# Feed-forward activations issued in another order, and attention keys written by two activations over all partitions

## The chip, the cores and the metric

The kernel runs on one core of a Trainium2 chip. The metric is the device time of one execution in microseconds (us), the median over several executions. One core has TensorE (matrix products into PSUM), VectorE, ScalarE (activations), GpSimd and DMA queues; each works through its own queue of instructions, and they wait for each other by semaphores. Profile lines call them PE, DVE, ACT and POOL; PEld is TensorE's loading of weights.

## The reference

128 graphs of 128 nodes with 256 features each go through two layers; everything is float32. Cut to what matters:

```python
# layer 0: two graph attention steps, then a feed-forward
def _gat(h, adj, W, a, out_features):
    Wh = jnp.matmul(h, W)
    e = jnp.matmul(Wh, a[:out_features]) + jnp.swapaxes(jnp.matmul(Wh, a[out_features:]), 1, 2)
    scores = jnp.where(adj > 0, jax.nn.leaky_relu(e, negative_slope=0.2), NEG)
    return jnp.matmul(jax.nn.softmax(scores, axis=1), Wh)

h = _gat(_gat(x, adj, W1, a1, 256), adj, W2, a2, 256)
h = _layernorm(x + h, g_ln1, b_ln1)
ff = jnp.matmul(jax.nn.relu(jnp.matmul(h, w_ff1) + b_ff1), w_ff2) + b_ff2     # 256 -> 1024 -> 256
src = _layernorm(h + ff, g_ln2, b_ln2)

# layer 1: attention of 8 heads of 32, values by relation r = 0..3, then a feed-forward
q, k = heads(src @ Wq + bq), heads(src @ Wk + bk)
attn = jax.nn.softmax(jnp.einsum('bhid,bhjd->bhij', q, k) / np.sqrt(32), axis=-1)
out = sum(jnp.einsum('bhij,bhjd->bhid', attn * (adj == r)[:, None], heads(src @ Wv[r] + bv[r])) for r in range(4))
x = _ln(src + out @ Wo + bo, g1, beta1)
ff = jax.nn.gelu(x @ W1 + b1, approximate=False) @ W2 + b2                   # 256 -> 1024 -> 256
return _ln(x + ff, g2, beta2)
```

## The kernel before

The 128 graphs go in 32 groups of 4. Each group passes through five stages (load, graph attention, feed-forward with Relu, attention, feed-forward with Gelu), and the stages of neighbouring groups are interleaved: each stage is a generator that yields an estimated duration, and a heap decides whose next piece is written into the program. The order of TensorE's instructions (and of the DMA queue's) is then fixed by added dependencies over most of the kernel; the orders on the other engines are chosen when the kernel is built, from the order of the program and from what is estimated to be ready.

PSUM holds eight buffers of 128x512 values; six are called `mm` and are used in turn by nearly all products.

```python
ps = ctx.enter_context(tc.tile_pool(name="ps", bufs=6, space=PSUM))
...
kbd = [cst.tile([P, G, 2, N], F32, name=f"kbd{c}") for c in range(DC)]
for c in range(DC):
    nc.gpsimd.memset(kbd[c], 0.0)
...
def normalised(y, first=0, n=G):          # layer norm without gain and offset
    ...                                   # VectorE: bn_stats, bn_aggr; GpSimd: rstd and -mean * rstd
    for b in range(n):
        nc.scalar.activation(y[:, b], y[:, b], AF.Identity, bias=nmr[:, b:b + 1], scale=rstd[:, b:b + 1])   # L235
```

The first product of the feed-forward is done with seven block products of Strassen-Winograd form for each half, in two units (`unit(0)`, `unit(2)`), each with four visits; `chain` and `side` are PSUM buffers, `lo` and `hi` hold the results and then the activations:

```python
def unit(f0):
    lo, hi = (wk.tile([P, 2, 2, T // 2], F32, name="fT", bufs=FC // 2) for _ in range(2))
    ...
    chain, side = (ps.tile([P, 2, T // 2], F32, name="mm") for _ in range(2))
    product(chain, 1, True)
    product(side, 5, True)                # products are L303
    nc.scalar.copy(lo[:, :, 0], chain)
    nc.scalar.copy(hi[:, :, 1], side)
    yield
    p = ps.tile([P, 2, T // 2], F32, name="mm")
    product(chain, 6)
    product(p, 2, True)
    product(side, 3)
    nc.scalar.copy(lo[:, :, 1], chain)
    nc.vector.tensor_add(lo[:, :, 0], lo[:, :, 0], p)             # L317
    nc.vector.tensor_add(lo[:, :, 1], lo[:, :, 1], side)          # L318
    yield
    product(chain, 7)
    nc.vector.tensor_add(hi[:, :, 1], hi[:, :, 1], chain)         # L321
    yield
    product(chain, 4)
    for i in range(2):
        nc.scalar.activation(lo[:, i], lo[:, i], func, bias=bin_[:, f0 + i:f0 + i + 1])        # L325
    for i in range(2):
        f = FC // 2 + f0 + i
        nc.scalar.activation(hi[:, i, 1], hi[:, i, 1], func, bias=bin_[:, f:f + 1])            # L328
        nc.scalar.activation(hi[:, i, 0], chain[:, i], func, bias=bin_[:, f:f + 1])            # L329
    yield

units = [unit(0), unit(2)]
for n, now in enumerate(((0,), (1,), (0,), (1,), (0,), (1,), (0,), (1,))):
    for u in now:
        next(units[u])
    ...
...
for b2_ in range(0, G, 2):                # the second product of the feed-forward
    p = ps.tile([P, 2, D], F32, name="mm")
    for b in (b2_, b2_ + 1):
        for n, f in enumerate(late):
            nc.tensor.matmul(p[:, b - b2_], fT[f][:, ts(b, N)], wout[:, f], ...)               # L346
    nc.vector.tensor_add(y[:, b2_:b2_ + 2], y[:, b2_:b2_ + 2], p)                              # L347
```

Other products that appear in the profile are L388 (features times weights) and L396, L406 (weighting) of the graph attention, L420 (queries), L426 (keys), L441 (scores), L474 (values), L486 (weighting by relation) and L524 (output) of the attention. L467 makes the masked weights on VectorE, L397 copies the four results of L396 out of PSUM on ScalarE, and L258 transposes on VectorE.

In the attention one score product takes two heads at once. For that the keys lie in `kbd` in a block form: of every two neighbouring heads of 32 rows, one fills slot 0 and the other slot 1, and the rows of the other head are zero there. The zeros are written once, at the start; each group writes only the rows of the heads, four activations of 32 partitions for each of the two halves `c`:

```python
for c in range(DC):
    p = ps.tile([P, G, N], F32, name="mm")
    for f in range(DC):
        nc.tensor.matmul(p, wkk[:, f, ts(c, P)], hT[:, :, f], start=f == 0, stop=f == DC - 1)      # L426
    for q in range(HC):
        rows = ts(q, DH)
        nc.scalar.activation(kbd[c][rows, :, q % 2], p[rows], AF.Identity, bias=bk[rows, c:c + 1])  # L429
...
def weights(b):
    scores = [ps.tile([P, DC, 2, N], F32, name="mm") for _ in range(2)]
    for c in range(DC):
        for h in range(2):
            rows = ts(h, P // 2)
            nc.tensor.matmul(scores[h][:, c], qT[rows, c, ts(b, N)], kbd[c][rows, b], ...)          # L441
```

A float32 matmul of the program stands as two instructions in the profile, so the four of `weights(b)` are eight there.

Of the kernel before, what the change touches and what calls it, by code (L numbers as in the profile page):

```python
# [12 lines left out]
F32 = mybir.dt.float32  # L13
I32 = mybir.dt.int32
AF = mybir.ActivationFunctionType
OP = mybir.AluOpType
# [6 lines left out]
P = 128  # L23
# [34 lines left out]
def graph_layers(ctx: ExitStack, tc: tile.TileContext, a: dict, out: bass.AP):  # L58
# [8 lines left out]
    nc = tc.nc  # L67
# [5 lines left out]
    DC = D // P  # L73
    FF = a["wf1"].shape[1]
    FC = FF // P
    R = a["wv"].shape[1] // D
    H = 8
    DH = D // H
    HC = P // DH
# [3 lines left out]
    cst = ctx.enter_context(tc.tile_pool(name="cst", bufs=1))  # L83
# [55 lines left out]
    for fc in range(DC):  # L139
        p = ps.tile([P, MW], F32, name="mm")  # L140
# [27 lines left out]
    bf1, b1, bq, bk = (at_col[k] for k in ("bf1", "b1", "bq", "bk"))  # L168

    def folded(w, bias, k, rows=False):  # L170

        gain, offset = at_col["g" + k], at_col["b" + k]
        if rows:
            for n in range(0, w.shape[-1], T):
                p = ps.tile([P, T], F32, name="mm")
                for c in range(DC):
                    nc.tensor.matmul(p, offset[:, c:c + 1].to_broadcast([P, P]), w[:, c, n:n + T],
                                     start=c == 0, stop=c == DC - 1)
                nc.vector.tensor_add(bias[:, n:n + T], bias[:, n:n + T], p)
        else:  # L180
            n = bias.shape[-1]
            p = ps.tile([P, n], F32, name="mm")
            for f in range(n):
                for c in range(DC):
                    nc.tensor.matmul(p[:, f:f + 1], w[:, c, ts(f, P)], offset[:, c:c + 1], start=c == 0, stop=c == DC - 1)
            nc.vector.tensor_add(bias, bias, p)
        for c in range(DC):
            nc.vector.tensor_scalar(w[:, c], w[:, c], gain[:, c:c + 1], None, op0=OP.mult)
# [21 lines left out]


    kbd = [cst.tile([P, G, 2, N], F32, name=f"kbd{c}") for c in range(DC)]
    for c in range(DC):
        nc.gpsimd.memset(kbd[c], 0.0)

    def per_row(v, n):

# [2 lines left out]
    def normalised(y, first=0, n=G):  # L220

        y = y[:, first:first + n]
        mv = sm.tile([P, n, 2], F32, name="mv")
        for b in range(n):
            st = sm.tile([P, 6], F32, name="st")
            nc.vector.bn_stats(st, y[:, b])  # L226
            nc.vector.bn_aggr(mv[:, b], st)
        rstd = sm.tile([P, n], F32, name="rstd")
        nc.gpsimd.tensor_scalar(rstd, mv[:, :, 1], EPS, None, op0=OP.add)
        nmr = sm.tile([P, n], F32, name="nmr")  # L230
        nc.gpsimd.tensor_scalar(nmr, mv[:, :, 0], -1.0, None, op0=OP.mult)
        nc.gpsimd.tensor_tensor(rstd, rstd, mhalf[:, :n], OP.pow)  # L232
        nc.gpsimd.tensor_mul(nmr, nmr, rstd)  # L233
        for b in range(n):
            nc.scalar.activation(y[:, b], y[:, b], AF.Identity, bias=nmr[:, b:b + 1], scale=rstd[:, b:b + 1])  # L235

    def affine(y, k, b, n, engine=nc.gpsimd):


        for op, v in zip((OP.mult, OP.add), ln[k]):  # L240
            engine.tensor_tensor(y[:, b:b + n], y[:, b:b + n], v[:, None, :].to_broadcast([P, n, D]), op)  # L241
# [26 lines left out]
    def features(y, direct):  # L268

        t = t_tile().rearrange("p (b c n) -> p b c n", b=G, c=DC)  # L270
        blocks = t.rearrange("p b c n -> p (b c) n")
        transposed(y.rearrange("p b (c f) -> p (b c) f", f=P), blocks, direct, blocks)
        return t

    def moving_sums(hT):

        b11, b21, b12, b22 = (hT[:, h:h + G // 2, c] for h in (0, G // 2) for c in range(DC))
        t1, t2, t4 = (wk.tile([P, G // 2, N], F32, name=f"t{i}") for i in (1, 2, 4))
        nc.gpsimd.tensor_sub(t1, b12, b11)  # L279
        nc.gpsimd.tensor_sub(t2, b22, t1)  # L280
        nc.gpsimd.tensor_sub(b12, b22, b12)
        nc.gpsimd.tensor_sub(t4, t2, b21)
        return None, b11, b21, b22, t4, t1, t2, b12

    def feed_forward(y, before, direct, win, bin_, wout, func, by=G):


        hT = features(y, direct)
        yield TIMES["lead ff0" if before == "01" else "lead ff1"]
        hs = moving_sums(hT)  # L290
        yield TIMES["sums"]
        fT = [None] * FC
# [5 lines that stand above are left out]
                fT[f0 + i] = lo[:, i].rearrange("p h t -> p (h t)")  # L298
                fT[FC // 2 + f0 + i] = hi[:, i].rearrange("p h t -> p (h t)")

            def product(p, k, first=False):
                for i in range(2):
                    nc.tensor.matmul(p[:, i], win[k][:, ts(f0 + i, P)], hs[k], start=first and i == 0, stop=True,  # L303
                                     skip_group_check=True)

            chain, side = (ps.tile([P, 2, T // 2], F32, name="mm") for _ in range(2))
            product(chain, 1, True)
            product(side, 5, True)
# [10 lines that stand above are left out]
            yield  # L319
            product(chain, 7)  # L320
            nc.vector.tensor_add(hi[:, :, 1], hi[:, :, 1], chain)  # L321
            yield
            product(chain, 4)
            for i in range(2):
                nc.scalar.activation(lo[:, i], lo[:, i], func, bias=bin_[:, f0 + i:f0 + i + 1])  # L325
            for i in range(2):
                f = FC // 2 + f0 + i
                nc.scalar.activation(hi[:, i, 1], hi[:, i, 1], func, bias=bin_[:, f:f + 1])  # L328
                nc.scalar.activation(hi[:, i, 0], chain[:, i], func, bias=bin_[:, f:f + 1])  # L329
            yield  # L330

        units = [unit(0), unit(2)]
# [3 lines that stand above are left out]
            if n in (2, 4):  # L336
                affine(y, before, n - 2, 2)
            yield TIMES["ff unit"]
        yield TIMES["ff2"]

        late = sorted(range(FC), key=lambda f: f % (FC // 2) // 2)
        for b2_ in range(0, G, 2):
# [3 lines that stand above are left out]
                    nc.tensor.matmul(p[:, b - b2_], fT[f][:, ts(b, N)], wout[:, f], start=n == 0, stop=n == FC - 1)  # L346
            nc.vector.tensor_add(y[:, b2_:b2_ + 2], y[:, b2_:b2_ + 2], p)  # L347
            yield TIMES["ff half"]
            if (b2_ + 2) % by == 0:
                normalised(y, b2_ + 2 - by, by)  # L350
        return y
# [59 lines left out]
    def attention(y, g, first, direct):  # L411
# [5 lines left out]
        for c in range(DC):  # L417
            p = ps.tile([P, T], F32, name="mm")
# [4 lines left out]
        for c in range(DC):  # L423
            p = ps.tile([P, G, N], F32, name="mm")
            for f in range(DC):
                nc.tensor.matmul(p, wkk[:, f, ts(c, P)], hT[:, :, f], start=f == 0, stop=f == DC - 1)  # L426
            for q in range(HC):
                rows = ts(q, DH)
                nc.scalar.activation(kbd[c][rows, :, q % 2], p[rows], AF.Identity, bias=bk[rows, c:c + 1])  # L429

        adj = ps.tile([P, G, N], F32, name="adj", bufs=1)
        nc.vector.tensor_copy(adj, at)
# [74 lines left out]
        for b in range(G):  # L507
# [8 lines left out]
            for k in range(0, 8, 2):  # L516
# [4 lines left out]
                if k == 4:  # L521
                    p = ps.tile([P, D], F32, name="mm")
# [37 lines left out]
    def stage_attention(g):  # L560
        if g == 0:
            folded(wq, bq, "02")
            folded(wkk, bk, "02")
            folded(wv_all, bv, "02", rows=True)
            folded(w1, b1, "11")
            later["w1"] = weight_sums(w1, "w1")
        x2[g] = yield from attention(x1.pop(g), g, g == 0, g == NG - 1)

    def stage_ff1(g):
# [8 lines left out]
        if not last:  # L578
            yield TIMES["store"]
            nc.sync.dma_start(out[g], y)  # L580

    stages = (stage_load, -75), (stage_gat, -39), (stage_ff0, 48), (stage_attention, 132), (stage_ff1, 300)
    todo = []
    for g in range(NG):
# [74 lines left out]
```

## Time and profile before

| | |
|---|---|
| time, median of 3 runs (lowest to highest) | 3239.61 us (3239.05 to 3241.12) |
| span of the profiled execution | 3241.0 us |
| mean granted TensorE clock | 0.991 of full speed |
| instructions | 55392 |
| L325, ScalarE, 128x512, x256 | 169.3 us busy, 709 ns each |
| L328, ScalarE, 128x256, x256 | 114.2 us busy, 493 ns each |
| L329, ScalarE, 128x256 from PSUM, x256 | 103.1 us busy, 465 ns each |
| L429, ScalarE, 32x512 from PSUM, x256 | 173.9 us busy, 679 ns each |
| table loads of ScalarE | 62, 1283 ns each |
| wait of L441's weight loads for L329, in total | 32.1 us |
| wait of L303 for VectorE's L321, in total | 18.2 us |

In lists of groups each line has the line of the kernel, the engine, what is written and what is read, the tile's shape and a count; then the total busy time and the mean of one. In a timeline each line has a start in us from the start of the span, a length in us, the engine, the line, the tiles and how many instructions were merged; what stands in square brackets is idle time of the engine just before, and what ended it. The chain that ended last is followed back from the last instruction: at each step to what released it, or to the instruction before it on its engine.

### The profile page before, as it was taken

What the parts mean: (1) busy time and instruction counts of PE and PEld (TensorE: products, weight loads), DVE (VectorE), ACT (ScalarE), POOL (GpSimd) and SP (SyncE); (2) the same over time, 40 slices, a digit from 0 to 9 for tenths busy, and PEclk for the clock granted to TensorE, in tenths of its full rate; (3) what the DMA queues carried; (4) which work ended last, traced back from release to release, by engine and by line L of the source; (5) the groups of instructions that cost most, each with busy time, mean ns of one, the idle gap of its engine ahead of it and who ended that gap; (6) DMA issues with size and microseconds to landing.
All of it is one profiled execution on the core that took longest, in us unless ns stands there. A gap on an engine that the chain in (4) does not pass through costs nothing.

```text
span 3241.0 us, 55392 instructions
## 1 busy us (share of the span) xinstructions
PE 3145.3 (97%) x20160; PEld 2383.3 (74%) x20160; DVE 2020.5 (62%) x3647; ACT 1766.8 (55%) x5191; POOL 1378.8 (43%) x1736
## 2 busy tenths in 40 slices
PE   7989999999999999999999999999999999999998
PEld 5756777777777777777777777777777777777766
DVE  3566566666566666576666576666576666666563
ACT  3545555565555565555565555565555565555543
POOL 2324345344345344345344345344345344344342
PEclk8999999999999999999999999999999999999999
DMA  4344454444454444454444454444453544453310
GB/s 152 68 102 98 102 117 101 105 98 98 100 119 102 104 95 100 99 121 96 111 94 97 103 120 97 110 92 98 105 121 89 117 92 98 104 115 85 85 33 14
DMA packets 1156400, 320.83 MB, mean 99 GB/s; under 512 B 902944, under 2 KB 1126688, under 8 KB 1156000
## 3 DMA queue, kind: packets, MB, share of 16 engines
q1 hardware_dynamic: 1156128, 317.29, 43.2%
q8 instruction: 160, 2.62, 0.3%
q14 instruction: 112, 0.92, 0.1%
HBM read 187.58 MB, written 129.62 MB: 98 GB/s over the span
## 4 chain that ended last, share of the span: by engine, by line
PE 75%; POOL 9%; ACT 7%; DVE 6%; DMA 1%; issue 1%; SPq 1%; ACTq 0%; POOLq 0%; DVEq 0%
PE mm L346 28%; PE mm L303 13%; PE mm L474 10%; PE av L486 5%; POOL tok L241 5%; PE mm L441 5%; PE mm L388 3%; PE mm L420 3%; PE mm L426 3%; PE mm L524 3%; ACT fT L325 2%; ACT tok L235 2%; POOL rstd L232 2%; PE mm L406 2%; DVE st L226 1%; ACT fT L328 1%
## 5 line engine op out<-in xcount | busy, mean ns | idle before, releaser
L467 DVE SCALAR_TENSOR_TENSOR m<-adj,eT 128x1024 f32<-128x1024 f32 x512 | 598.8, 1213 | 228.5 <-DMA eT<-zd 161.9
L241 POOL TENSOR_TENSOR tok<-tok,ln_rows 128x512 f32<-128x512 f32 (+1 forms) x636 | 668.7, 1060 | 42.1 <-PE mm L252 14.8
L453 POOL TENSOR_TENSOR e<-e,s 128x512 f32<-128x512 f32 x256 | 266.1, 1040 | 706.2 <-DVE s L452 679.0
L451 ACT ACTIVATE e<-mm,nm 128x128 f32<-128x128 f32 x1024 | 360.7, 376 | 190.0 <-DVE nm L447 167.2
L474 PE MATMUL mm<-wv,T 128*128 128x512 f32 x1024 | 464.2, 596 | 0.0
L346 PE MATMUL mm<-wf,fT 128*128 128x256 f32 x2048 | 456.9, 381 | 0.0
L346 PE MATMUL mm<-w,fT 128*128 128x256 f32 x2048 | 455.5, 381 | 0.2 <-DVE v L475 0.2
L346 PEld LDWEIGHTS mm<-w,fT 128*128 128x128 f32 x2048 | 386.6, 190 | 74.6 <-issue 23.8
L346 PEld LDWEIGHTS mm<-wf,fT 128*128 128x128 f32 x2048 | 386.4, 190 | 63.3 <-ACT wh L397 9.3
L235 ACT ACTIVATE tok<-tok,nmr,rstd 128x256 f32<-128x256 f32 x512 | 269.4, 594 | 178.7 <-POOL nmr L233 166.2
L474 PEld LDWEIGHTS mm<-wv,T 128*128 128x128 f32 x1024 | 191.5, 190 | 199.6 <-issue 189.3
L347 DVE TENSOR_TENSOR tok<-tok,mm 128x512 f32<-128x512 f32 x128 | 87.8, 686 | 351.5 <-PE mm L346 351.5
L486 PE MATMUL av<-m,v 128*32 128x128 f32 x8192 | 254.8, 276 | 8.8 <-DVE v L475 4.9
L486 PEld LDWEIGHTS av<-m,v 128*32 128x32 f32 x8192 | 218.8, 111 | 54.3 <-issue 41.6
L429 ACT ACTIVATE kbd<-mm,col 32x512 f32<-32x512 f32 x256 | 173.9, 679 | 151.0 <-PE mm L426 147.0
L377 POOL TENSOR_TENSOR e<-e,s 128x512 f32<-128x512 f32 x64 | 66.5, 1039 | 432.7 <-DVE s L376 338.4
L279 POOL TENSOR_TENSOR t<-T 128x256 f32<-128x256 f32 x64 | 46.4, 726 | 466.7 <-DMA T<-zd 466.7
L451 ACT ACTIVATION_READ_ACCUMULATOR e<-mm,nm 128x1 f32 x1024 | 219.8, 215 | 0.0
L447 DVE TENSOR_REDUCE nm<-mm 128x4 f32<-128x512 f32 x256 | 162.9, 675 | 64.5 <-PE mm L441 64.5
L303 PE MATMUL mm<-T,w 128*128 128x256 f32 x768 | 197.0, 386 | 0.2 <-ACT T L256 0.2
L475 DVE TENSOR_TENSOR v<-mm,bv 128x512 f32<-128x512 f32 x256 | 167.5, 684 | 46.8 <-PE mm L474 46.8
L303 PE MATMUL mm<-T,wf 128*128 128x256 f32 x768 | 192.6, 380 | 0.0
(121 smaller groups left out, 5112.3 us busy)
## 6 DMA issues: line engine op xcount, KB each, us to landing
zd<-e SPq DMA_DIRECT2D x496, 128.0 KB, 3.1
eT<-zd SPq DMA_DIRECT2D x124, 512.0 KB, 4.0
zd<-T SPq DMA_DIRECT2D x364, 128.0 KB, 3.5
T<-zd SPq DMA_DIRECT2D x91, 512.0 KB, 3.9
xt<-in_xT_dram SPq DMA_DIRECT2D x32, 512.0 KB
at<-in_adjT_dram SPq DMA_DIRECT2D x64, 256.0 KB, 6.1
tok<-in_x_dram SPq DMA_DIRECT2D x32, 512.0 KB
out_dram<-tok SPq DMA_DIRECT2D x31, 512.0 KB, 6.5
```

Source lines behind the costliest of these rows:

```text
L235: nc.scalar.activation(y[:, b], y[:, b], AF.Identity, bias=nmr[:, b:b + 1], scale=rstd[:, b:b + 1])
L241: engine.tensor_tensor(y[:, b:b + n], y[:, b:b + n], v[:, None, :].to_broadcast([P, n, D]), op)
L303: nc.tensor.matmul(p[:, i], win[k][:, ts(f0 + i, P)], hs[k], start=first and i == 0, stop=True, skip_group_check=True)
L346: nc.tensor.matmul(p[:, b - b2_], fT[f][:, ts(b, N)], wout[:, f], start=n == 0, stop=n == FC - 1)
L429: nc.scalar.activation(kbd[c][rows, :, q % 2], p[rows], AF.Identity, bias=bk[rows, c:c + 1])
L447: nc.vector.tensor_reduce(nm, p, AX.X, OP.max, negate=True)
L451: nc.scalar.activation(eh[:, q], p[:, q], AF.Exp, bias=nm[:, q:q + 1], accum_out=s[:, q:q + 1])
L453: nc.gpsimd.tensor_mul(eh, eh, per_row(s, N))
L467: nc.vector.scalar_tensor_tensor(m, ab, r, eT, op0=OP.is_equal, op1=OP.mult)
L474: nc.tensor.matmul(p, hT[:, b, f], wv[:, f, r:r + 2], start=f == 0, stop=f == DC - 1)
L475: nc.vector.tensor_add(v[:, r:r + 2].rearrange("p r d -> p (r d)"), p.rearrange("p r d -> p (r d)"), bv[:, r * D:(r + 2) * D])
L486: last = nc.tensor.matmul(po[ts(q, DH), c], v[:, r, c * P + q * DH:c * P + (q + 1) * DH], ms[r][:, q // 2 * HC + c * 2 + q % 2], start=r = ...
```

## The change

There are two parts. In the feed-forward's units the activations of `lo` move from the last visit to the one before it, and in the last visit the two activations that read the PSUM buffer `chain` come ahead of the two that read `hi[:, :, 1]` from SBUF. This is for the PSUM buffers to come free earlier. In the attention each half of the keys is written by two activations over all 128 partitions, one for each slot, in place of four over 32. A scale of 1 or 0 for each partition (`own`) keeps the rows of the slot's own heads and writes zeros to the others; the bias is multiplied by the same numbers beforehand (`bk_own`). So the memsets of `kbd` at the start are not needed.

```diff
     kbd = [cst.tile([P, G, 2, N], F32, name=f"kbd{c}") for c in range(DC)]
-    for c in range(DC):
-        nc.gpsimd.memset(kbd[c], 0.0)
+
+    own = cst.tile([P, 2], F32, name="own")
+    nc.vector.memset(own, 0.0)
+    for q in range(HC):
+        nc.vector.memset(own[ts(q, DH), q % 2:q % 2 + 1], 1.0)
+    bk_own = [cst.tile([P, DC], F32, name=f"bk{q}") for q in range(2)]
...
             product(chain, 7)
             nc.vector.tensor_add(hi[:, :, 1], hi[:, :, 1], chain)
+            for i in range(2):
+                nc.scalar.activation(lo[:, i], lo[:, i], func, bias=bin_[:, f0 + i:f0 + i + 1])
             yield
             product(chain, 4)
-            for i in range(2):
-                nc.scalar.activation(lo[:, i], lo[:, i], func, bias=bin_[:, f0 + i:f0 + i + 1])
-            for i in range(2):
-                f = FC // 2 + f0 + i
-                nc.scalar.activation(hi[:, i, 1], hi[:, i, 1], func, bias=bin_[:, f:f + 1])
-                nc.scalar.activation(hi[:, i, 0], chain[:, i], func, bias=bin_[:, f:f + 1])
+            for h, p in enumerate((chain, hi[:, :, 1])):
+                for i in range(2):
+                    f = FC // 2 + f0 + i
+                    nc.scalar.activation(hi[:, i, h], p[:, i], func, bias=bin_[:, f:f + 1])
             yield
...
-            for q in range(HC):
-                rows = ts(q, DH)
-                nc.scalar.activation(kbd[c][rows, :, q % 2], p[rows], AF.Identity, bias=bk[rows, c:c + 1])
+            for q in range(2):
+                nc.scalar.activation(kbd[c][:, :, q], p, AF.Identity, scale=own[:, q:q + 1], bias=bk_own[q][:, c:c + 1])
...
             folded(wkk, bk, "02")
+            for q in range(2):
+                nc.vector.tensor_scalar(bk_own[q], bk, own[:, q:q + 1], None, op0=OP.mult)
```

## The prediction

> **What bounds the kernel now.** I read the shares of the engines first, then the table of 100 us stretches, then the chain that ended last over two rounds of the loop, and only then the instructions of single engines around the places where that chain leaves TensorE.
>
> ```profile
> PE 3145.3 (97%) x20160; PEld 2383.3 (74%) x20160; DVE 2020.5 (62%) x3647; ACT 1766.8 (55%) x5191; POOL 1378.8 (43%) x1736
> ```
>
> TensorE is the engine that is nearly full. From 300 us to 3000 us each 100 us shows it 98.2 to 98.9% busy at a granted clock of 1.00, so the middle of the kernel is one pattern. One group of four graphs passes every 97.48 us: the first score product after the feed-forward stands at 911.85, 1009.33 and 1106.81 us in the chain.
>
> The busy share hides something, since the ends of matmuls are modelled. The chain shows what. In order of time (start, length in us, engine, line), one round:
>
> ```profile
> 1078.41 7.12 PE mm L346 x32
> ...
> 1086.16 1.21 DVE e L370
> ...
> 1090.18 1.04 POOL e L377
> ...
> 1099.73 0.17 POOL nmr L233
> ...
> 1099.92 2.08 ACT tok L235 x4
> 1102.00 1.22 ACT fT L325 x2
> 1103.22 0.80 ACT fT L328 x2
> 1104.02 1.23 ACT fT L325 x2
> 1105.25 0.80 ACT fT L328 x2
> 1106.05 0.72 ACT fT L329 x2
> ...
> 1106.81 0.70 PE mm L441 x2
> ...
> 1107.53 1.13 PE mm L441 x6
> ```
>
> The reader should see that from the end of L346 at 1085.53 to L441 at 1106.81, 21.28 us, the chain is not on TensorE. It goes through VectorE, GpSimd's part of the layer norms, four normalising activations (L235) and ten of the feed-forward's twelve activations. TensorE works beside it, but not for the whole time. Its own instructions there:
>
> ```profile
> 1100.77 1.97 PE L303 MATMUL mm<-t,wf 128*128 128x256 f32 x8 [0.59 <-DVE fT L321]
> 1102.57 1.90 PE L396 MATMUL mm<-wh,e 128*128 128x258 f32 x8
> 1104.40 1.96 PE L486 MATMUL av<-m,v 128*32 128x128 f32 x64
> 1106.81 1.85 PE L441 MATMUL mm<-kbd,T 64*128 64x256 f32 x8 [0.46 <-ACT fT L329]
> ```
>
> Two stalls. (a) L441: L486 takes 1.89 us where nothing stops it, so L441 could start at 1106.29; it starts at 1106.81 (0.52 us), and takes 1.85 us where two undisturbed occurrences in this round take 1.06 (0.79 us more, between its first output and its second). Together 1.31 us; one round earlier 0.28 + 0.79 = 1.07. (b) The last product of the feed-forward (L303 from t and wf): the 8 matmuls of L474 before it start at 1096.58 and take 3.43, so it could start at 1100.01 and starts at 1100.77: 0.76 us, one round earlier 0.99. Both rounds lose 2.07 us, so the round needs 97.48 - 2.07 = 95.41 us of TensorE.
>
> The reason for (a) is in the code. PSUM has six "mm" buffers. Two units' `chain` and four outputs of L396 fill them, and the two score outputs of L441 take the buffers that the two `chain` give back, which L329 reads last of all twelve activations.
>
> The reason for (b) is VectorE's order; its instructions ahead of it are:
>
> ```profile
> 1094.19 0.69 DVE L317 TENSOR_TENSOR fT<-fT,mm 128x512 f32<-128x512 f32 x1 [0.22 <-PE mm L303]
> 1094.81 4.62 DVE L467 SCALAR_TENSOR_TENSOR m<-adj,eT 128x1024 f32<-128x1024 f32 x4
> 1099.35 0.68 DVE L318 TENSOR_TENSOR fT<-fT,mm 128x512 f32<-128x512 f32 x1
> 1099.94 1.28 DVE L321 TENSOR_TENSOR fT<-fT,mm 128x512 f32<-128x512 f32 x2
> ```
>
> Four masks of attention (4.62 us) stand between the units' additions, so L321, which must read `chain` before the last product adds to it, is late.
>
> **What the Trainium skill says.** "Perfetto Trace Analysis", section "Identifying the Most-Contended Engine", says that matmul busy share is no good measure of how near TensorE is to its limit. The trace agrees: 98.9% busy, but 2.07 of 97.48 us lost. The same page, "Optimization Strategy", says that a gap which repeats can mean too little PSUM for the next tile; (a) is that, 1.07 to 1.31 us a round. "PSUM — Partial Sum Buffer", section "Engine vs sequencer instructions", says that ScalarE's and VectorE's queues are strict FIFO. The trace agrees: L325, whose inputs were there by 1100.03, starts at 1101.90 behind L235. "ScalarE: Activation LUTs", section "What ACT_TABLE_LOAD costs", gives about 280 ns + 0.833 ns an element per lane with a bias operand, and some 93 ns more for a second per-partition operand; 128x512 should be 707 ns, and L325 has 709. L235 (scale and bias, 128x256) has 594 against 493 of L328 (bias alone), 101 ns more.
>
> **The change part by part.**
>
> *Activations of lo one visit ahead.* The four L325 depend on L317 and L318, done at about 1093.9 for the first unit and 1100.0 for the second, not on the last product. ScalarE idles 2.24 us before the L235 of 1096.15 and 1.69 us before that of 1099.92. Two L325 (1.22) fit into the first gap, or all four go in front of L329. Work removed: none. Work moved off the path between L235 and L329: 1.22 to 2.45 us.
>
> *Chain first.* In the trace the second unit's L325 and L328 run before the first unit's L329, against the order of the program; so ScalarE's order is set when the kernel is built, by what is thought ready. I can't read from the diff the order that will come out. With L235 ending at 1102.00 and the last product's first half at about 1101.8, L329 of the first unit can end at 1102.75 at best; with two L325 and two L328 still ahead of it, at 1104.8; the second's 1.5 to 2 us later at most. L441 wants its buffers at 1106.29 and half a microsecond later. Stall (a) goes in all these orders: 1.07 to 1.31 us a round. Should none of L325 move ahead of L235, the twelve activations and the first copy of L397 still have to run before L346 finds a buffer: 1102.00 + 5.4 + 0.4 = 1107.8 instead of the 1108.66 at which it starts now; then 0.9 us are left.
>
> *Keys by two activations instead of four.* Eight of 679 ns on 32 partitions become four on 128 partitions with a scale operand; time goes by elements per lane, so I estimate 679 + 101 = 780 ns. A group: 5.56 us to about 3.1, or 2.4 us of ScalarE (79 us in all, off a 55% engine). In the steady rounds the keys end at 1069.62 and are first read at 1074.33, so 4.7 us of slack hide it. Only at the start, where the chain runs through L429 from 202.80 to 208.36, are the 2.4 us on the path, once. The two memsets that go (1.84 us on GpSimd at 0.86 us) stand beside loads, and the five small memsets and two products that come are on VectorE in the head: 0.
>
> *Sum.* Stall (b) stays, as VectorE's queue from L347 (released by the end of L346) to L321 is untouched: new round 95.41 + (0.76 to 0.99) = 96.2 to 96.4, 1.2 us less. L441 meets this chain from 326.95 to 2958.97 us, 27 rounds and so 28 stalls: 28 x 1.2 = 33.6 us. The list of waits agrees in size: weight loads of L441 waited 32.1 us in total for L329. With the head's 2.4: 3239.6 - 33.6 - 2.4 = 3203.6, say 3204.
>
> **Rivals.**
>
> *The saved time comes back at L321.* If stall (b) grew by what (a) loses, the time would stay at 3237. Against it: (b) starts from L347, which waits for TensorE itself (1.19 us idle before it), and the masks' inputs have no wait in this round, so the queue moves ahead with TensorE. For it: masks waited 161.9 us in total for their DMA elsewhere.
>
> *An early L325 delays L235.* The second unit's L325 can't run before 1100.0; queued ahead of the L235 of 1099.92 it pushes that, and the transpose on VectorE that waits for it, by 1.3 to 2.5 us. VectorE has 2.20 us idle before its next mask at 1105.77. In the Gelu half the L235 of 1047.41 and the transposes stand ahead of L321 at 1050.69, and the product that needs it starts at 1054.37, with some 2 us to spare. If both margins broke by half a microsecond: 28 x 1.0 lost, about 3230. A Gelu moved in between exponentials would cost two table loads of 1283 ns more a round; but the last exponential before it is at 1039.70 and the next after 1074, so I don't expect it.
>
> *Both stalls go.* If the new order at build time also puts L321 ahead of the masks, 28 x 2.07 = 58 us and the head's 2.4: 3179. Nothing in the diff asks for it.
>
> **Range and chances.** The floor in sight is 3179, the ceiling no gain at 3237 or a few more for a less lucky order in the head, whose first 300 us aren't the pattern. 8 in 10: 3184 to 3234. Faster by over 2% means under 3174.8, below the floor: 0.04. Slower by over 2% needs 2.3 us more a round, for which I see no cause: 0.02. Within 2%: 0.94.
>
> **What would show it.** Right: a round of about 96.3 us; L441's wait for L329 near 0; L329 ended before L486 ends; at least two L325 ahead of the last product; L321's wait still 0.6 us a round; the keys' activations at about 780 ns x128. Wrong: a round of 97.5 with a larger wait at L303 (first rival), waits of L258 for L235 above 1.5 us and new stalls behind them (second), or a changed order on VectorE.

## The result, and the profile after

| | before | after |
|---|---|---|
| time, median of 4 runs each (lowest to highest) | 3240.36 us (3239.05 to 3242.64) | 3209.11 us (3208.02 to 3210.72) |
| ratio after to before, 95% interval | | 0.9903 (0.9886 to 0.9920) |
| span of the profiled execution | 3241.0 us | 3208.9 us |
| granted clock | 0.991 | 0.989 |
| round of the steady part, median | 97.48 us | 96.24 us |

The change takes 31 us off. The prediction was 3204 us, with a range of 3184 to 3234.

The lines of the changed kernel have other numbers. The products: L303 is now L307, L346 is L350, L396 is L400, L441 is L444, L474 is L477, L486 is L489. On VectorE: L317 is L321, L318 is L322, L321 is **L325**, L467 is L470. On ScalarE: L235 is L239, the activations of `lo` are L327 (before L325), those of `hi[:, :, 1]` and of `chain` are both L333 (told apart by what they read: `fT` or `mm`), the keys are L432.

The shares of the engines after:

```profile
PE 3124.8 (97%) x20160; PEld 2377.2 (74%) x20160; DVE 2019.9 (63%) x3654; ACT 1688.2 (53%) x5063; POOL 1377.3 (43%) x1734
```

ScalarE does 78.6 us less (1766.8 - 1688.2); the keys alone take 81.4 less (173.9 before, 92.5 now). TensorE has the same 20160 instructions. The share doesn't say where the 31 us are from; the chain that ended last does. A piece of one round after (start, length in us, what):

```profile
1461.92 7.78 PE mm L307 x36
...
1469.74 3.48 DVE m L470 x3
1473.21 0.59 DVE fT L322
1473.81 0.61 DVE fT L325
...
1474.55 1.97 PE mm L307 x8
...
1480.14 1.10 PE mm L444 x8
```

Before, the chain left TensorE for 21.28 us a round and came back at the score product by way of GpSimd and ScalarE. Now it leaves only for the 4.85 us from 1469.70 to 1474.55, for three masks, the second unit's addition and L325, and comes back at the last product of the feed-forward (L307 at 1474.55): the prediction's stall (b). The score product takes 1.10 us where it took 1.85.

ScalarE's instructions in one Relu half, after:

```profile
1082.26 1.33 ACT L327 ACTIVATE fT<-fT,col 128x512 f32<-128x512 f32 x2
1084.41 2.08 ACT L239 ACTIVATE tok<-tok,nmr,rstd 128x256 f32<-128x256 f32 x4 [0.81 <-POOL nmr L237]
1088.19 2.07 ACT L239 ACTIVATE tok<-tok,nmr,rstd 128x256 f32<-128x256 f32 x4 [1.70 <-POOL nmr L237]
1090.17 1.32 ACT L327 ACTIVATE fT<-fT,col 128x512 f32<-128x512 f32 x2
1091.39 1.69 ACT L333 ACTIVATE fT<-fT,col 128x256 f32<-128x256 f32 x4
1092.99 1.53 ACT L333 ACTIVATE fT<-mm,col 128x256 f32<-128x256 f32 x4
```

Two of the four L327 (the first unit's) run in the gap ahead of the normalising L239, where before all four came behind. The second unit's two now also run ahead of the first unit's two of `hi`. Nothing else changed in the order of this half. (In the Gelu half the four L327 now run together, ahead of a copy; TensorE's products beside them have no wait, before or after.) The activations that read `chain` (fT<-mm) still come last: written first in the program, they came out of the build last; that what is ready earlier is put ahead of them is inferred from the orders, no run shows it by itself. On TensorE, VectorE, GpSimd and the DMA queue the orders of the steady rounds are those of before.

TensorE's two places in that round:

```profile
1089.01 1.97 PE L307 MATMUL mm<-t,wf 128*128 128x256 f32 x8 [0.57 <-DVE fT L325]
...
1094.53 1.16 PE L444 MATMUL mm<-kbd,T 64*128 64x256 f32 x8
```

The wait for VectorE is what it was (0.59 before, 0.57 after), and the score product waits for nothing. Its weight loads still wait 0.2 us a round for L333 (6.1 us in total, 32.1 before), which doesn't hold it up.

### The profile page after: what moved, and what is told of

The parts are those of the page before. It is cut to its first block, busy times and chain, and to the rows that moved or that the text cites. A ratio compares the mean times of both kernels' runs of the same rounds, so it can differ in the third digit from the quotient of the medians.

```text
span 3208.9 us, 55180 instructions
## 1 busy us (share of the span) xinstructions
PE 3124.8 (97%) x20160; PEld 2377.2 (74%) x20160; DVE 2019.9 (63%) x3654; ACT 1688.2 (53%) x5063; POOL 1377.3 (43%) x1734
## 4 chain that ended last, share of the span: by engine, by line
PE 58%; DVE 4%; DMA 1%; issue 0%; ACT 0%; POOL 0%; SPq 0%; ACTq 0%; POOLq 0%; DVEq 0%
PE mm L350 18%; PE mm L307 15%; PE mm L477 7%; PE av L489 5%; DVE m L470 3%; PE mm L444 3%; PE mm L527 2%; PE mm L430 2%; PE mm L424 2%; PE mm L392 2%; PE mm L400 1%; PE mm L410 1%; DVE fT L325 0%; DVE fT L322 0%; DMA eT<-zd 0%
## 5 line engine op out<-in xcount | busy, mean ns | idle before, releaser
L470 DVE SCALAR_TENSOR_TENSOR m<-adj,eT 128x1024 f32<-128x1024 f32 x512 | 598.8, 1213 | 242.5 <-DMA eT<-zd 176.9
L477 PE MATMUL mm<-wv,T 128*128 128x512 f32 x1024 | 464.2, 596 | 0.0
L350 PE MATMUL mm<-wf,fT 128*128 128x256 f32 x2048 | 456.9, 381 | 0.0
L350 PE MATMUL mm<-w,fT 128*128 128x256 f32 x2048 | 455.5, 381 | 1.1 <-DVE v L478 1.1
L350 PEld LDWEIGHTS mm<-w,fT 128*128 128x128 f32 x2048 | 386.6, 190 | 75.5 <-issue 23.8
L350 PEld LDWEIGHTS mm<-wf,fT 128*128 128x128 f32 x2048 | 386.4, 190 | 63.3 <-ACT wh L401 8.9
L239 ACT ACTIVATE tok<-tok,nmr,rstd 128x256 f32<-128x256 f32 x512 | 269.2, 594 | 137.7 <-POOL nmr L237 125.1
L477 PEld LDWEIGHTS mm<-wv,T 128*128 128x128 f32 x1024 | 191.5, 190 | 199.6 <-issue 189.3
L489 PE MATMUL av<-m,v 128*32 128x128 f32 x8192 | 256.2, 277 | 8.1 <-DVE v L478 4.2
L489 PEld LDWEIGHTS av<-m,v 128*32 128x32 f32 x8192 | 219.8, 111 | 54.1 <-issue 42.2
L307 PE MATMUL mm<-T,w 128*128 128x256 f32 x768 | 196.5, 385 | 0.2 <-ACT T L260 0.2
L307 PE MATMUL mm<-T,wf 128*128 128x256 f32 x768 | 192.6, 380 | 0.0
L373 ACT ACTIVATE e<-e,wh 128x128 f32<-128x128 f32 x240 | 77.3, 408 | 210.2 <-DMA e<-zsd 210.2
```

Of the source, the lines that this page charges most:

```text
L470: nc.vector.scalar_tensor_tensor(m, ab, r, eT, op0=OP.is_equal, op1=OP.mult)
L477: nc.tensor.matmul(p, hT[:, b, f], wv[:, f, r:r + 2], start=f == 0, stop=f == DC - 1)
L489: last = nc.tensor.matmul(po[ts(q, DH), c], v[:, r, c * P + q * DH:c * P + (q + 1) * DH], ms[r][:, q // 2 * HC + c * 2 + q % 2], start=r = ...
```

## The experiments

The questions were which of the three edits made the gain, whether stall (a) was really one of PSUM buffers, and what sets the round now. Beside each time stands the round, the distance between two starts of the last product of the Relu feed-forward in the trace, the median over the 27 steady rounds. Most rounds repeat within some hundredths of a us, so they tell more than the whole time, to which the head and the end of the kernel add some us of their own.

**Which edit.** Three runs, with 3241.05 us for the kernel before beside them.

Run with lo put back into the last visit:

```diff
             nc.vector.tensor_add(hi[:, :, 1], hi[:, :, 1], chain)
-            for i in range(2):
-                nc.scalar.activation(lo[:, i], lo[:, i], func, bias=bin_[:, f0 + i:f0 + i + 1])
             yield
             product(chain, 4)
+            for i in range(2):
+                nc.scalar.activation(lo[:, i], lo[:, i], func, bias=bin_[:, f0 + i:f0 + i + 1])
```

> The changed kernel with the activations of lo put back into the last visit; chain still ahead of hi, keys still by two activations. My theory: ScalarE's queue in the Relu half is then as in the kernel before (all activations of SBUF operands ahead of those of chain, all behind the normalising ones), so both stalls stay, the round is 97.5 us and only the head gains 2 to 3 us: about 3238. If putting chain first in the program were what gained, 3209 to 3212.

Measured: 3244.08 us, ratio 1.0007 (0.9998 to 1.0016), round 97.50. ScalarE's order in the Relu half is that of before.

Run with lo one visit ahead as the only edit of the kernel before (the same lines moved the other way).

> The kernel before with the activations of lo one visit ahead, nothing else. My theory: the first unit's two activations go ahead of the normalising ones, the stall of the score product goes, the round is 96.2 to 96.3 us, and only the head's 2 to 3 us are missing: about 3211. If the keys or chain first are needed for it, 3225 to 3240.

Measured: 3207.87 us, ratio 0.9898 (0.9883 to 0.9913), round 96.28. The wait of the score product's weight loads for L329, 32.1 us in total before, is 0.8.

Run with the keys by two activations as the only edit of the kernel before (the diff's parts on `kbd`, `own` and `bk_own`).

> The kernel before with the keys by two activations, nothing else. My theory: ScalarE is relieved of some 80 us, nearly all of it off the path; the head gains 2 to 3 us, the round stays 97.48: about 3238. If relieving ScalarE were what gained, 3209 to 3220.

Measured: 3243.24 us, ratio 1.0009 (1.0000 to 1.0017), round 97.46.

So the gain is the move of `lo` and nothing else. The 81.4 us that the keys take off ScalarE are worth nothing in the time, and the order of `chain` and `hi` in the program changed nothing, since it didn't change the order on the engine. The head's 2.4 us are missing in the run of the keys. The start of its attention shows why. Before, then keys only (TensorE):

```profile
206.16 0.70 PE L441 MATMUL mm<-kbd,T 64*128 64x256 f32 x4
207.01 0.70 PE L441 MATMUL mm<-kbd,T 64*128 64x256 f32 x2 [0.15 <-ACT kbd L429]
208.41 0.70 PE L441 MATMUL mm<-kbd,T 64*128 64x256 f32 x2 [0.70 <-ACT kbd L429]
...
212.28 1.13 PE L524 MATMUL mm<-wo,oT 128*128 128x256 f32 x4 [0.22 <-ACT oT L490]
```

```profile
206.35 1.13 PE L444 MATMUL mm<-kbd,T 64*128 64x256 f32 x8
...
211.46 1.13 PE L527 MATMUL mm<-wo,oT 128*128 128x256 f32 x4 [1.02 <-ACT oT L493]
```

The waits for the keys are gone, but at the very next product 0.8 us come back as a wait for another result of ScalarE (1.02 instead of 0.22), and by the first steady round nothing is left: from the third to the fourth last product it is 155.99 us with the keys alone and 155.61 before.

**Is it the PSUM buffers?** In the kernel before, the two activations of `chain` were made to run ahead of those of `hi`, by a dependency on ScalarE's order (shortened):

```diff
-            for i in range(2):
-                f = FC // 2 + f0 + i
-                nc.scalar.activation(hi[:, i, 1], hi[:, i, 1], func, bias=bin_[:, f:f + 1])
-                nc.scalar.activation(hi[:, i, 0], chain[:, i], func, bias=bin_[:, f:f + 1])
+            for h, p in enumerate((chain, hi[:, :, 1])):
+                for i in range(2):
+                    f = FC // 2 + f0 + i
+                    now = nc.scalar.activation(hi[:, i, h], p[:, i], func, bias=bin_[:, f:f + 1])
+                    if h:      # order alone, no wait
+                        tc.add_manual_dep(now.ins, first, NoSync, reason="chain first")
+                    else:
+                        first = now.ins.name
```

> The kernel before with an added dependency on ScalarE alone, so that in each unit the two activations of chain really run ahead of the two of hi; lo stays in the last visit and the keys by four activations. My theory (the score product waits for the PSUM buffers of chain): all twelve activations still run behind the normalising ones, chain is freed at about 3.2 and 4.8 us after them instead of 4.8 and 5.5, and the stall of the score product nearly goes; then the second feed-forward product has to wait some 0.4 us for the first copy of the graph attention's results: 0.8 to 0.9 us a round are won, round 96.6, about 3216. If it were not the buffers of chain but the count of activations behind the normalising ones, nothing: 3240.

Measured: 3228.75 us, ratio 0.9962 (0.9947 to 0.9977), round 96.66. ScalarE and TensorE in one round of it:

```profile
1103.79 2.54 ACT L325 ACTIVATE fT<-fT,col 128x512 f32<-128x512 f32 x4
1106.24 0.81 ACT L329 ACTIVATE fT<-mm,col 128x256 f32<-128x256 f32 x2
1106.96 0.90 ACT L329 ACTIVATE fT<-fT,col 128x256 f32<-128x256 f32 x2
1107.75 0.82 ACT L329 ACTIVATE fT<-mm,col 128x256 f32<-128x256 f32 x2
```

```profile
1108.18 1.57 PE L446 MATMUL mm<-kbd,T 64*128 64x256 f32 x8
```

The same twelve activations stand behind the normalising ones as before; only what reads `chain` is earlier, and 0.82 us a round go. So the release of `chain` is what the score product waited for. Here it starts without a wait and takes 1.57 us (1.85 before, 1.06 undisturbed), as the second unit's `chain` is still read late. The whole time is 13 us above what was expected, for the most part because the order was forced at the start too: there the first steady round begins 8.4 us later (329.32 instead of 320.88).

A second test gave TensorE a seventh buffer. For that the relation matrix was kept in SBUF as bytes; a control does the same but leaves six buffers:

```diff
-    ps = ctx.enter_context(tc.tile_pool(name="ps", bufs=6, space=PSUM))
+    ps = ctx.enter_context(tc.tile_pool(name="ps", bufs=7, space=PSUM))     # control: 6
...
-        adj = ps.tile([P, G, N], F32, name="adj", bufs=1)
+        adj = wk.tile([P, G, N], mybir.dt.uint8, name="adj", bufs=1)
```

> The kernel before with the relation matrix of attention kept in SBUF as bytes instead of PSUM, and its PSUM bank given to the common buffers: seven instead of six. Activations are untouched. My theory: the score product waits for PSUM buffers. Its first output finds the seventh, its second needs the first unit's chain, given back just in time: stall (a) of 1.07 to 1.31 us a round nearly goes with ScalarE's order as before, round 96.3 to 96.6, 3211 to 3220 (if the masks take no longer, which the next run shows). If the activations delay something else than buffers, 3240.

> Control to the run with seven buffers: the relation matrix in SBUF as bytes, but six common buffers as before; all engines' orders are as before. If the masks take no longer from SBUF, 3240 and the same stalls; each 10 ns more a mask would be 40 ns more for the last product's wait a round.

Measured: seven buffers 3401.34 us, ratio 1.0496 (1.0480 to 1.0511), round about 102.2; control 3414.61 us, ratio 1.0537 (1.0521 to 1.0553), rounds of 102.7 to 104.4. Both expectations fail by far, for a reason that has nothing to do with buffers (below). Against its control the seventh buffer shortens TensorE's waits for L329 at the score product from 102.8 to 58.2 us in total and the round by some 1.2 us (on average 102.1 instead of 103.3). That fits, but the orders on VectorE and GpSimd differ between the two as well, so it shows less than the run with the forced order.

**What sets the round now?** The prediction left stall (b) to VectorE's order. In this run of the changed kernel two of the four masks are written into the program 5 us later:

```diff
+LATER = 5
...
             by_relation(0, eT[0], ms, PARTS[k // 2:k // 2 + 1])
-            yield TIMES["mask0"]
+            yield LATER if k == 2 else 0
         for b in range(G):
             affine(y, "02", b, 1)
-            yield TIMES["av"]
+            yield TIMES["av"] - (0 if b else LATER)
```

> The changed kernel with two of the first graph's four masks written into the program 5 us later, so that VectorE makes two masks, then the second unit's addition and the two L321, then the other two masks. TensorE's and ScalarE's orders are those of the changed kernel. My theory: the wait of the last feed-forward product for L321 (0.6 to 0.8 us a round) is only VectorE's order; it goes, TensorE's own work of 95.41 us sets the round but for some 0.3 us at the score product, as ScalarE's part now ends last: round 95.4 to 95.8, 27 rounds of 0.45 to 0.85 us less, 3186 to 3197. Rival: the time comes back at once at the score product or at the weighting that reads the later masks, round 96.2, 3209.

Measured: 3211.19 us, ratio 0.9909 (0.9894 to 0.9924), round 96.24, the same as the changed kernel. The rival was right, though the time came back at another place than it named. TensorE in one round (L308 is the last product, L401 the graph attention's weighting):

```profile
1090.49 1.89 PE L308 MATMUL mm<-t,wf 128*128 128x256 f32 x8
1092.22 1.47 PE L401 MATMUL mm<-wh,e 128*128 128x258 f32 x6
1094.26 0.70 PE L401 MATMUL mm<-wh,e 128*128 128x258 f32 x2 [0.57 <-ACT fT L334]
```

L308 no longer waits. But the fourth output of L401 does (28 times, 15.9 us in total), for a `chain` that ScalarE has yet to read: VectorE now takes the second result of the values out of PSUM behind two masks and a transposition, at 1093.57 us, so one of the six buffers is missing earlier. It is stall (a) again, at an earlier product. So both had to go at once. With the forced order of `chain` and `hi` added to the split masks:

> The kernel with split masks, and on ScalarE the activations of chain forced ahead of those of hi in each unit. My theory: what is left at the score product in the run before goes too, but the first copy of the graph attention's results is as late as there; round 95.4 to 95.6, 3186 to 3192. If ScalarE's end of the chain isn't what is left there, the same as the run with split masks alone.

Measured: 3201.71 us, ratio 0.9883 (0.9866 to 0.9899), round 95.41. The weighting's wait for ScalarE is gone, and the round is the 95.41 us that the prediction worked out as TensorE's own work; the whole time is 10 to 16 us above what was expected, again by a late first steady round (329.47). The next run forces the order only in the Relu half of the fourth to the last but one group. Beside it ran the counterpart, the changed kernel with the same forced order but the masks left together, and the changed kernel once more.

> Split masks, and chain forced ahead of hi on ScalarE only in the Relu half of the groups from the fourth to the last but one; the head keeps the order of the run with split masks alone. The run with it everywhere had rounds of 95.41 us but lost 9 to 11 us before its first steady round. My theory: first steady round at 320 to 321 us, rounds of 95.4, 27 of them 0.83 us shorter than the changed kernel's 96.24, so 3187 to 3191. Rival: the head's loss isn't from the forced order, then 3198 to 3202.

> The changed kernel, and in the Relu half of the same groups chain forced ahead of hi on ScalarE; masks as in the changed kernel. My theory: the changed kernel's round of 96.24 is set by VectorE's L321, not by ScalarE, so nothing is won: round 96.2, 3205 to 3211. If ScalarE still set the round, 95.4 and 3187.

> The changed kernel once more, on the same chip as the two before: rounds of 96.24, 3209, and a first steady round and an end that differ from the first profile by up to 2 us, as the loads at the start and the DMA round trips at the end don't repeat exactly.

Measured beside 3242.57 us for the kernel before: both 3190.54 us, ratio 0.9840 (0.9826 to 0.9855), round 95.42, first steady round at 319.40; forced order alone 3210.32 us, ratio 0.9898 (0.9882 to 0.9915), round 96.22; the changed kernel again 3207.89 us, ratio 0.9894 (0.9879 to 0.9909), round 96.27. TensorE in one round of the run with both (L497 is the weighting by relation, L452 the scores):

```profile
1083.35 1.89 PE L308 MATMUL mm<-t,wf 128*128 128x256 f32 x8
...
1087.14 1.95 PE L497 MATMUL av<-m,v 128*32 128x128 f32 x64 [0.16 <-DVE v L486]
1089.03 1.14 PE L452 MATMUL mm<-kbd,T 64*128 64x256 f32 x8
```

What is left is some 0.2 us at L497 for the values, so TensorE's own work is nearer to 95.2 us than to 95.41 by this estimate. Each of the two edits alone leaves the round at 96.2; together they take off another 0.82 us, and the kernel is 17 us faster than the changed one that ran beside it (3190.54 and 3207.89; 20.5 in the profiled spans).

## Why the prediction was right

- **Bound and stalls.** Right. The round was set by the way over GpSimd and ScalarE to the score product, and with both stalls gone the round is 95.42 for a predicted 95.41; as 0.2 us of that are a wait, the stalls had been taken a little too small, and that the hundredths agree is luck.
- **lo one visit ahead.** Right, in the order that was named first: two L325 in the first gap, the rest behind. Stall (a) went and stall (b) stayed, with a new round of 96.24 for a predicted 96.2 to 96.4. 27 rounds of 1.21 us (the mean; the medians differ by 1.24) are 32.7 us; the prediction took 33.6 (28 times 1.2).
- **Chain first.** The prediction left open which order would come out. It had no effect in the steady rounds (round 97.50 without the move of lo). The 0.9 us that it kept for the case in which nothing moves ahead of L235 would have been 0.82 with `chain` really first.
- **Keys.** The duration was right (773 ns for an estimated 780), as was the slack in the steady rounds. **The head's 2.4 us failed.** That they were on the path was read from the chain; what came next on that path was not followed, and so it was taken for granted that they stay won. The waits for the keys did go (the next score product begins 2.95 us after the first instead of 4.76, 1.8 us earlier), and were spent again at the next waits; nothing of them is left at 320 us.
- **Where the other 4 us are.** Predicted 35.6 off, measured 31.3 (32.1 in the profiled spans). 32.7 are in the rounds. At the first steady round the changed kernel is 2.0 us ahead. Of these, 1.9 are there when TensorE first begins L388, now L392 (18.57 instead of 20.44): the 32 products of one column ahead of it (L185) take 5.10 us instead of 6.99. In the repeated profile of the changed kernel they take 4.74, but 6.99 again in the run with the order forced on the changed kernel, whose program is the same up to there. So this can't be laid to the change; why they differ was not settled. Behind the last steady round the changed kernel loses 2.6 us, though the last of the 28 stalls lay there too. In good part it loses them in DMA round trips that did not get shorter with the rest (VectorE waits 2.41 us for a transposed weight where it waited 0.66). The repeated profile of the same kernel lost 1.3 there, and the run with `lo` alone won 1.5. What of it is the change and what differs from run to run was not settled.
- **Rivals.** "The saved time comes back at L321" didn't happen: its wait is 0.57 a round. "An early L325 delays L235" didn't either: VectorE's transposes wait 40.6 us in total for L239 where they waited 41.1 for L235, and the table loads are 62 as before. "Both stalls go" didn't happen with this change, and the floor of 3179 given for it was too low by some 11 us, since the run that removes both has 3190.5.

## What to carry to other kernels

Follow the chain of one round from where it leaves the full engine to where it comes back, and look at what stands in the queue between: here two activations that nobody waited for, ahead of those whose end gave PSUM buffers back. An instruction written earlier in the program only helps if the order on the engine changes by it, so read that order first. When two paths of nearly the same length hold up one engine, as GpSimd with ScalarE and VectorE do here after the change, shortening one shows nothing until the other is shortened too; TensorE's own work per round, added up from undisturbed lengths, tells how much is left.

## What the runs showed of the hardware

Keeping the relation matrix in SBUF was expected to cost some ns a mask. The masks went from 1213 to 1347 ns on average, but GpSimd's small instructions beside them got many times longer, and with them the layer norms on the way to the score product. GpSimd in one round of the control, while VectorE makes four masks from 1144.45 to 1149.39:

```profile
1144.99 1.09 POOL L229 TENSOR_SCALAR rstd<-mv 128x4 f32<-128x4 f32 x1
1146.16 1.05 POOL L231 TENSOR_SCALAR nmr<-mv 128x4 f32<-128x4 f32 x1
1147.18 1.14 POOL L233 TENSOR_TENSOR nmr<-nmr,rstd 128x4 f32<-128x4 f32 x1
```

In the kernel before, the same three stand beside masks with one operand in PSUM (1094.81 to 1099.43):

```profile
1095.41 0.23 POOL L229 TENSOR_SCALAR rstd<-mv 128x4 f32<-128x4 f32 x1
1095.72 0.23 POOL L231 TENSOR_SCALAR nmr<-mv 128x4 f32<-128x4 f32 x1
1095.92 0.20 POOL L233 TENSOR_TENSOR nmr<-nmr,rstd 128x4 f32<-128x4 f32 x1
```

In the control each lasts about as long as a mask: the two engines take turns. Ahead of the masks, at 1140.89 in the same round, L229 takes 0.23 us there too. The Trainium skill's "SBUF — State Buffer", section "Who interferes with whom", says that a VectorE instruction with two SBUF inputs contends with a GpSimd one that reads SBUF, and the trace agrees: over the whole kernel L229 has 233 ns on average before and 630 ns in the control. The run changed the type of the operand together with its place, so no run here separates the two. The round grows by 5 to 7 us by it, for a mask that is 134 ns longer. Part of that is TensorE's own: in this round it waits 3.68 us for L329 at the score product, and the 32 products of L346 behind it take 8.22 us where they took 7.17, with a granted clock of 0.68 from 1162 to 1166 us; it was 1.00 at that place of the kernel before. In the other rounds of the control these 32 products take 7.9 to 9.6 us. So the PSUM bank that looked like a spare buffer is, as far as these runs show, what kept the two engines apart.
